# A two-layer graph kernel in fp32 on one core: first slot with zero matmuls ahead of x, second halves of the first rows earlier, and the last statistics in another order

## The chip, the core and the metric

One Trainium2 chip, one of its cores. The time is device microseconds from start to end of one execution; the figure of a kernel is the median of its runs. For the kernel before it is 1274.52 us (three runs, 1274.45 to 1275.23).

## What is computed

The input is `x` (16 x 1024 x 256, fp32) and a symmetric 0/1 matrix `adj` for each of the 16 batches (1024 x 1024). Two layers follow one another, and each ends in a residual sum and a layer norm:

```
e      = leaky(einsum('bid,bjd->bij', x * a0, x))        # slope 0.2
alpha  = where(adj == 1, sigmoid(e), 0)                  # a1..a3 serve adj == 2, 3, 4
x      = layernorm(x + einsum('bij,bjd->bid', alpha, x) + bias)

H      = x @ W
e      = where(adj != 0, exp(-leaky(s[n] + d[m])), 0)    # s = H a_src, d = H a_dst
x      = layernorm(x + elu((e @ H) / rowsum(e)))
```

The kernel has a pass for adjacency of zeros and ones, `one_kind_pass`, which also gathers a flag, and a general pass that only runs if the flag says that another value occurred. With these inputs the general pass does not run.

## The kernel before, in words

**Tiling.** One batch is a slot. A slot's 1024 rows are eight tiles of 128 rows (`NT = 8`), its 256 features two halves of 128 (`ND = 2`), its 1024 columns two halves of 512 (`HALF`). Everything on TensorE is fp32. The order of the instructions on each engine is that of the text: `tc.manual_schedule()` (line 83) leaves no scheduler to move them. Each engine works through its own queue in order, so a waiting instruction holds up what stands behind it.

**Layer 0 of a slot.** `transpose_x` (191) or a blocked load with `turn_x` (184) gives `xT` (features on partitions) and `xa = xT * a0`. For each row tile `jt`, `strip` (205) makes the scores of the tile against the columns from its own on (`pe`, line 219), ScalarE takes tanh twice (227, 228: sigmoid is written as tanh), VectorE takes the larger (229). `finish` (231, the operation is line 235) adds 1, multiplies by the adjacency and writes `al`; POOL puts the diagonal in (245). Since scores and adjacency are symmetric, the part below the diagonal is not computed: in slot 0 `mirror` (268) transposes the blocks on TensorE and VectorE masks them (276). `multiply0` (325, matmul at 332) sums `al` times `x` for one tile of 128 columns of `al`; column tiles 0 to 3 read only the first 512 columns of `al`, tiles 4 to 7 the second 512. `end0` (340) adds the bias and takes the statistics of the layer norm.

**Slot 0's order (504 to 540).** `x` comes in four DMAs, groups of two row tiles: groups 0 and 2 on the SP queue, 1 and 3 on ScalarE's. `a0` comes as a column, 256 elements of 4 bytes, on SP (137), then bias, `a` and `W` (159 to 165), and `x` of slot 1 on SP (513). POOL's queue has four DMAs for the adjacency of slot 0 (quarters: column half by row half) and two for that of slot 1. In `transpose_x` TensorE turns a block into `pxT` (200), VectorE copies it to `xT` (202), ScalarE makes `xa` out of the same PSUM tile (203). Then follow `strip` 0, 1, 2 with `finish` and `mirror` for the first 512 columns, and the loop over eight column tiles `t`: `multiply0(t)`, `strip(t+3)`, `finish(t+2)`, `mirror(t+2)`, then for `t < 4` `finish(0, t, HALF, N)`, the second half of row tile `t`, and `end0(t)`. `make_Wx` (167) in `t = 0, 1` reads `a` and `W`; the blocked load of slot 1's `xT` goes into the same tile as `a` and so waits for it.

**Slots 1 to 15 (542 to 635).** Layer 0 of slot `b` runs beside layer 1 of slot `b-1`: `project` (395), `weights` (439), `sum1` (446), `elu` and `add` (454 to 489).

**The end (638 to 763).** Layer 1 of slot 15. The first three tiles of the result are stored from line 747, tiles 3 and 4 from 753. The last three, 5, 6 and 7 (`N_LAST = 3`), lie in `y_last` and are stored behind the branch on the flag (1108, 1109) in two DMAs on SP: tile 5, then tiles 6 and 7. Tile 7 is made in two half tiles (`end_half`, 705). For tiles 6 and 7 the root is taken on ScalarE (`root`, 641), which loads a table for it, and is inverted with one Newton step on VectorE (646 to 651); two VectorE operations (760) scale the tiles. The statistics of tile 6 are ended by `bn_aggr` in `stats` (288), called from `add` (481) at line 733, ahead of the half tiles of tile 7; those of tile 7 at line 755.

Of the kernel before, what the change touches and what calls it, by code (L numbers as in the profile page):

```python
# [9 lines left out]
F32 = mybir.dt.float32  # L10
# [3 lines left out]
AF = mybir.ActivationFunctionType  # L14
ALU = mybir.AluOpType
# [3 lines left out]
P = 128  # L19
HALF = 512  # L20
# [3 lines left out]
EPS = 1e-5  # L24
LOW = 1.0e-14
CHECKS = 4
N_LAST = 3


@with_exitstack  # L30
def one_kind_pass(
# [33 lines left out]
    nc = tc.nc  # L65
    B, N, D = x.shape
    NT = N // P
    ND = D // P
    HT = HALF // P
    assert ND == 2 and NT == 8 and HT == 4 and N_LAST == 3  # L70

    TINY = 1.0e-36
    const = ctx.enter_context(tc.tile_pool(name="const", bufs=1))
    four = ctx.enter_context(tc.tile_pool(name="four", bufs=4))
    one = ctx.enter_context(tc.tile_pool(name="one", bufs=1))
# [12 lines left out]
    def load_x(b, queues):  # L88
        xs[b] = two.tile([P, NT, D], F32, tag="x", name=f"x_{b}")
        rows = x[b].rearrange("(t p) d -> p t d", p=P)  # L90
        n = NT // len(queues)
        for g, queue in enumerate(queues):
            queue.dma_start(xs[b][:, ts(g, n), :], rows[:, ts(g, n), :])
# [37 lines left out]
        )  # L131


    load_x(0, [nc.sync, nc.scalar, nc.sync, nc.scalar])
    acol = const.tile([P, ND], F32, tag="acol", name="acol")
    with nc.allow_non_contiguous_dma(reason="a column of 256"):
        nc.sync.dma_start(acol, a0.rearrange("(c p) o -> p (c o)", p=P))
    ident = const.tile([P, P], F32, tag="ident", name="ident")
    make_identity(nc, ident)
    ident2 = const.tile([P, P], F32, tag="ident2", name="ident2")  # L140
# [10 lines left out]
    for h in range(2):  # L151
        for g in range(2):
            load_adj(0, g, ts(h, HALF))
    for g in range(2):
        load_adj(1, g)
    power = const.tile([P, NT], F32, tag="power", name="power")
    nc.gpsimd.memset(power, -0.5)
    bias_bc = const.tile([P, D], F32, tag="bias", name="bias_bc")
    nc.sync.dma_start(bias_bc, bias.partition_broadcast(P))

    y_kept = const.tile([P, NT, D], F32, tag="y", name="y_kept")
    a_bc = y_kept[:, 0:2, :].rearrange("p t d -> p (t d)")
    nc.sync.dma_start(a_bc, a[0].partition_broadcast(P))
    Wx = const.tile([P, ND, D + 2], F32, tag="Wx", name="Wx")
    nc.sync.dma_start(Wx[:, :, 2:], W.rearrange("(c p) o -> p c o", p=P))

    def make_Wx(c):

        for s in range(2):
# [21 lines left out]
    def transpose_x(b, g):  # L191

        if g == 0:
            new_xT(b)
            xas[b] = one.tile([P, ND, N], F32, tag="xa", name=f"xa_{b}")
        for c in range(ND):
            pool, tag = ((ps_t, "t"), (ps_acc, "acc"), (ps_acc if c else ps_e, "acc" if c else "e"), (ps_t, "t"))[g]
            pt = pool.tile([P, 2, P], F32, tag=tag, name=f"pxT_{b}_{g}_{c}")
            for t in range(2):
                nc.tensor.transpose(pt[:, t, :], xs[b][:, 2 * g + t, ts(c, P)], ident)  # L200
            flat = pt.rearrange("p t q -> p (t q)")
            nc.vector.tensor_copy(xTs[b][:, c, ts(g, 2 * P)], flat)
            nc.scalar.mul(xas[b][:, c, ts(g, 2 * P)], flat, acol[:, c : c + 1])

    def strip(b, jt):

# [78 lines left out]
    def stats(y, mv, what):  # L285
        st = small.tile([P, nc.vector.BN_STATS_DIM], F32, tag="st", name=f"st_{what}")
        nc.vector.bn_stats(st, y)  # L287
        nc.vector.bn_aggr(mv, st)  # L288

    def rstd(mv, what):  # L290

# [189 lines left out]
    def add(b, t, between=None):  # L481

        y = ys[b][t]
        nc.vector.scalar_tensor_tensor(y, y, 1.0, hs[b, t], ALU.min, ALU.add)
        if (b, t) != (B - 1, NT - 2):
            nc.vector.scalar_tensor_tensor(y, y, -1.0, x1s[b][:, t, :], ALU.add, ALU.add)
        if between:
            between()
        stats(y, mv1s[b][:, t, :], f"1_{b}_{t}")

    def scale1(b, t):
        scale(ys[b][t], *r1s[b][t])

    def store(b, t0, n):
        rows = out[b].rearrange("(t p) d -> p t d", p=P)
        nc.sync.dma_start(rows[:, ds(t0, n), :], y_of[b][:, ds(t0, n), :])

    def acc1(b, t, pool, tag):
        return pool.tile([P, D + 1], F32, tag=tag, name=f"acc1_{b}_{t}")
# [3 lines left out]

    for g in range(NT // 2):
        transpose_x(0, g)
    strip(0, 0)
    strip(0, 1)
    for jt in range(2):
        finish(0, jt, 0, HALF)
        mirror(0, jt)  # L510
        if jt == 0:
            strip(0, 2)
    load_x(1, [nc.sync])
    for t in range(NT):
        multiply0(0, t)
        if t + 3 < NT:
            strip(0, t + 3)
        if t < 2:
            finish(0, t + 2, 0, HALF)
        elif t + 2 < NT:  # L520
            finish(0, t + 2)
        if t + 2 < NT - 1:
            mirror(0, t + 2)
        if t < HT:
            finish(0, t, HALF, N)
        end0(0, t)
        if t < 2:
            make_Wx(t)
        if t == 1:
            new_xT(1)  # L530
            load_blocks(xTs[1], x[1], 0, N)
        if 1 <= t <= CHECKS:
            check_adj(0, t - 1)
        if t in (4, 5):
            scale0(0, 2 * t - 8)
            scale0(0, 2 * t - 7)
            turn_x(1, t - 4)
        if t == 5:
            save_x1(0, 0)
            fetch_x1(0, 0)  # L540
# [97 lines left out]
    last, done = B - 1, B - 2  # L638
    r1s[last] = []

    def root(t):

        v = mv1s[last][:, t : t + 2, 1]
        r = const.tile([P, 2], F32, tag="root", name="root")
        nc.scalar.activation(r, v, AF.Sqrt, bias=eps)  # L645
        nc.vector.reciprocal(r, r)

        n = const.tile([P, 2], F32, tag="newton", name="newton")
        nc.vector.scalar_tensor_tensor(n, v, EPS, r, ALU.add, ALU.mult)
        nc.vector.scalar_tensor_tensor(n, n, -0.5, r, ALU.mult, ALU.mult)  # L650
        nc.vector.scalar_tensor_tensor(r, n, 1.5, r, ALU.add, ALU.mult)
        return r

    n_first = 4
    first = [acc1(last, t, *((ps_e, "e") if t < 3 else (ps_t, "t"))) for t in range(n_first)]
    for m in range(NT):
# [61 lines left out]
    for t in range(end):  # L718
        if n_first - 1 <= t < end - 1:
            multiply1(t + 1)  # L720
        if t == 5:
            multiply_halves()
        if t == 4:
            total = ps_t.tile([P, HT, P], F32, tag="t", name="total")[0:1, 0, 0:1]
            nc.tensor.matmul(total, lhsT=any_bad, rhs=ones, start=True, stop=True)
        elu(last, t, accs[t])
        if 1 <= t < 6:
            add(last, t - 1)
        if t == 5:
            nc.vector.tensor_copy(flag, total)  # L730
            add(last, t)
        if t == 6:
            add(last, t, invert)
        if t in (4, 5):
            r1s[last] += center(mv1s[last][:, ds(3 * t - 12, 3), :], f"1_{last}_{t}")
        if t == 5:
            n_bad = nc.values_load(
                flag, min_val=0, max_val=P, skip_runtime_bounds_check_because="a number of partitions"
            )
        for q in range(2 * t - 4, 2 * t - 2) if 2 <= t < 6 else []:  # L740
            scale1(done, q)
            if q in (3, 7):
                store(done, q - 3, HT)
        if t == 5:
            for q in range(3):
                scale1(last, q)
            store(last, 0, 3)
# [4 lines left out]
    scale1(last, 4)  # L752
    store(last, 3, 2)
    end_half(1)
    nc.vector.bn_aggr(mv1s[last][:, end, :], st_end)
    r = root(6)
    scale1(last, 5)
    for q in (6, 7):
        y = ys[last][q]
        nc.vector.tensor_scalar(  # L760
            y, y, mv1s[last][:, q, 0:1], r[:, q - 6 : q - 5], ALU.subtract, ALU.mult
        )
# [313 lines left out]
def kernel(  # L1076
    tc: tile.TileContext,
    x: bass.AP,
    adjT: bass.AP,
    a0: bass.AP,  # L1080
    a1: bass.AP,
    a2: bass.AP,
    a3: bass.AP,
    bias: bass.AP,
    W: bass.AP,
    a: bass.AP,
    out: bass.AP,
):

    nc = tc.nc
    B, N = x.shape[0], x.shape[1]
    NCHK = B * CHECKS
    with tc.tile_pool(name="flag", bufs=1) as flagp:
        chk = flagp.tile([P, NCHK], F32, tag="chk", name="chk")  # L1100
        fit = flagp.tile([P, B], F32, tag="fit", name="fit")
        y_last = flagp.tile([P, N_LAST, x.shape[2]], F32, tag="y_last", name="y_last")
        n_bad = one_kind_pass(tc, x, adjT, a0, bias, W, a, out, chk, fit, y_last)
        with tc.If(n_bad > 0) as found:
            general_pass(tc, x, adjT, a0, a1, a2, a3, bias, W, a, out)
        with found.Else():
            rows = out[B - 1].rearrange("(t p) d -> p t d", p=P)
            for t, n in ((0, 1), (1, 2)):
                nc.sync.dma_start(rows[:, ds(N // P - N_LAST + t, n), :], y_last[:, ds(t, n), :])


# [35 lines left out]
```

## Time and profile before

| | value |
|---|---|
| median of three runs | 1274.52 us |
| the profiled execution, its own time | 1274.88 us |
| its span, first to last instruction | 1272.9 us |
| TensorE matmuls busy | 1259.1 us (99%) |
| weight loads | 1023.2 us (80%) |
| VectorE | 925.1 us (73%) |
| ScalarE | 651.7 us (51%) |
| POOL | 293.1 us (23%) |
| first matmul starts at | 4.57 us |
| last matmul ends at | 1264.97 us |
| HBM | 151.91 MB read, 60.62 MB written |

The profile comes from one execution. Its own time, 1274.88 us, is 0.36 us above the median of the runs, and 2.0 us of it lie outside the span. In the lines below a matmul in fp32 is two records of the trace, a transpose on TensorE is one. "PEld" is the loading of the stationary operand, which goes on beside a matmul. In a line of the timeline the first number is the start, the second the busy time, in us, `x16` the number of instructions merged into the line; in brackets stands the idle time of the engine ahead of it and what ended it. `SPq`, `ACTq` are a queue issuing DMAs. Matmuls overlap: a record lasts longer than the distance to the next, so the distance is the figure to work with.

### The profile page before, as it was taken

The numbers are of one execution on the slowest core, as the hardware profiler recorded it, in microseconds if no ns is written. First come the engines' busy times: TensorE is split into PE (matmuls) and PEld (weight loads), VectorE is DVE, ScalarE is ACT, GpSimd is POOL, SyncE is SP. The second block draws the span as 40 slices with busy tenths as digits, with TensorE's granted clock in tenths as the row PEclk, the third lists the DMA queues.
The fourth block names the chain that finished last, engine by engine and source line by source line (L and its number), as shares of the span: only waits on it lengthen the run. The fifth ranks groups of instructions, "written<-read, shape, count | busy, mean of one in ns | idle before, by whom it ended". The sixth has DMA issues, their size and how long they took to land.

```text
span 1272.9 us, 17479 instructions
## 1 busy us (share of the span) xinstructions
PE 1259.1 (99%) x5469; PEld 1023.2 (80%) x5469; DVE 925.1 (73%) x2015; ACT 651.7 (51%) x1467; POOL 293.1 (23%) x592
## 2 busy tenths in 40 slices
PE   8999999999999999999999999999999999999997
PEld 6788787887878878788787887878778787887886
DVE  4685877858678686876868868687686867858657
ACT  4544544456454563545645445454455645456434
POOL 2212231212312133121222212223112231212203
PEclk9999999999999999999999999999999999999999
DMA  9379494895948859597694966959579594895312
GB/s 214 72 169 153 87 204 86 179 177 104 192 89 180 170 105 195 92 173 165 131 196 86 179 138 136 194 99 182 119 167 184 99 198 87 176 179 103 100 34 69
DMA packets 604452, 180.24 MB, mean 142 GB/s; under 512 B 481992, under 2 KB 586944, under 8 KB 604352
## 3 DMA queue, kind: packets, MB, share of 16 engines
q1 hardware_dynamic: 583216, 137.03, 54.1%
q0 software_dynamic: 20592, 41.48, 18.3%
q8 instruction: 46, 0.75, 0.2%
q10 hardware_dynamic: 544, 0.52, 0.1%
q14 instruction: 54, 0.44, 0.1%
HBM read 151.91 MB, written 60.62 MB: 167 GB/s over the span
## 4 chain that ended last, share of the span: by engine, by line
PE 98%; DVE 1%; ACT 0%; DMA 0%; issue 0%; ACTq 0%; DVEq 0%
PE acc L332 35%; PE acc L446 34%; PE pe L219 20%; PE pH L395 9%; DMA x<-in_x 0%; PE pxT L200 0%; PE pal L274 0%; PE prow L421 0%; PE pp L414 0%; DVE al L235 0%; ACT y L315 0%; ACT y_kept L315 0%; ACT L645 0%; PE px1T L378 0%; DVE st L287 0%
## 5 line engine op out<-in xcount | busy, mean ns | idle before, releaser
L332 PE MATMUL acc<-x,al 128*128 128x256 f32 x2048 | 445.8, 379 | 1.2 <-DVE al L235 1.2
L446 PE MATMUL acc<-H,e 128*128 128x257 f32 x2032 | 445.3, 380 | 0.0
L446 PEld LDWEIGHTS acc<-H,e 128*128 128x128 f32 x2032 | 384.7, 190 | 57.3 <-DVE e L439 0.6
L332 PEld LDWEIGHTS acc<-x,al 128*128 128x128 f32 x2048 | 387.4, 190 | 53.4 <-DVE al L235 1.6
L219 PE MATMUL pe<-xa,xT 128*128 128x384 f32 (+1 forms) x720 | 251.4, 486 | 0.0
L219 PEld LDWEIGHTS pe<-xa,xT 128*128 128x128 f32 x720 | 133.0, 190 | 81.1 <-issue 42.9
L315 ACT ACTIVATE x<-x,mr,r 128x256 f32<-128x256 f32 x128 | 69.4, 592 | 225.1 <-POOL mr L311 225.1
L439 DVE SCALAR_TENSOR_TENSOR e<-p,pq,adj 128x1024 f32<-128x1024 f32 x128 | 159.7, 1269 | 22.9 <-DMA p<-p_row 19.9
L294 POOL TENSOR_SCALAR ve<-mv 128x4 f32<-128x4 f32 (+2 forms) x49 | 16.8, 344 | 662.9 <-DVE mv L288 658.9
L478 ACT ACTIVATE h<-acc,rinv 128x256 f32<-128x256 f32 x126 | 59.2, 470 | 204.7 <-DVE rinv L470 189.1
L227 ACT ACTIVATE tb<-pe 128x512 f32<-128x512 f32 (+1 forms) x192 | 94.2, 491 | 121.9 <-PE pe L219 93.4
L469 DVE TENSOR_SCALAR rinv<-acc 128x1 f32<-128x1 f32 x127 | 20.0, 157 | 161.9 <-PE acc L446 161.8
L229 DVE TENSOR_TENSOR tb<-tb,low 128x512 f32<-128x512 f32 (+1 forms) x192 | 103.3, 543 | 42.2 <-ACT low L228 42.1
L124 ACT ACTIVATE junk<-adj,minus 128x2048 bf16<-128x2048 bf16 x64 | 127.3, 1989 | 0.0
L395 PE MATMUL pH<-Wx,x1T 128*128 128x258 f32 x512 | 126.3, 381 | 0.0
L395 PEld LDWEIGHTS pH<-Wx,x1T 128*128 128x128 f32 x512 | 97.2, 190 | 35.8 <-issue 14.3
L245 POOL TENSOR_TENSOR al<-ident,al 128x128 f32<-128x128 f32 x128 | 67.8, 530 | 230.4 <-DVE al L235 230.1
L235 DVE SCALAR_TENSOR_TENSOR al<-tb,adj 128x512 f32<-128x512 f32 (+7 forms) x132 | 97.7, 740 | 5.0
L266 DVE SCALAR_TENSOR_TENSOR al<-al,adj 128x512 f32<-128x512 f32 (+3 forms) x150 | 76.9, 537 | 24.2 <-DMA al<-mir 24.2
L228 ACT ACTIVATE low<-pe 128x512 f32<-128x512 f32 (+1 forms) x192 | 93.0, 485 | 0.5 <-DVE tb L229 0.5
L342 DVE SCALAR_TENSOR_TENSOR x<-acc,bias_bc 128x256 f32<-128x256 f32 x128 | 53.8, 420 | 43.7 <-PE acc L332 43.6
L251 DVE STREAM_TRANSPOSE tb<-tb 128x896 f32<-128x896 f32 (+6 forms) x105 | 74.7, 712 | 3.6
(99 smaller groups left out, 942.7 us busy)
## 6 DMA issues: line engine op xcount, KB each, us to landing
adj<-in_adjT POOLq DMA_DIRECT2D x30, 1024.0 KB, 10.1
x_rows<-x SPq DMA_DIRECT2D x31, 512.0 KB, 3.8
x1T<-x_rows SPq DMA_DIRECT2D x248, 64.0 KB, 2.5
x<-in_x SPq DMA_DIRECT2D x15, 1024.0 KB, 6.4
out<-y_kept SPq DMA_DIRECT2D x30, 512.0 KB, 6.6
xT<-in_x SPq DMA_DIRECT2D x112, 128.0 KB, 4.6
p<-p_row POOLq DMA_DIRECT2D x15, 512.0 KB, 4.6
mir<-tb SPq DMA_DIRECT2D x60, 112.0 KB, 3.0
```

Source lines behind the costliest of these rows:

```text
L124: nc.scalar.activation(junk, rows, AF.Square, bias=minus1, scale=2.0, accum_out=chk[:, b * CHECKS + n : b * CHECKS + n + 1],)
L219: nc.tensor.matmul(pe[:, 0:w], lhsT=xTs[b][:, c, ts(jt, P)], rhs=xas[b][:, c, ds(jt * P + o, w)], start=(c == 0), stop=(c == ND - 1),)
L227: nc.scalar.activation(tb[:, ds(o, w)], pe[:, 0:w], AF.Tanh, scale=0.5)
L228: nc.scalar.activation(low[:, 0:w], pe[:, 0:w], AF.Tanh, scale=0.5 * SLOPE)
L229: nc.vector.tensor_tensor(tb[:, ds(o, w)], tb[:, ds(o, w)], low[:, 0:w], ALU.max)
L235: nc.vector.scalar_tensor_tensor(als[b][:, jt, c0:c1], tbs[b, jt][:, c0 - jt * P : c1 - jt * P], 1.0, adjs[b, jt // HT][:, jt % HT, c0:c1] ...
L251: nc.vector.transpose(tb, tb)
L266: nc.vector.scalar_tensor_tensor(v, v, 1.0, rows, ALU.add, ALU.mult)
L332: nc.tensor.matmul(acc, lhsT=als[b][:, jt, ts(t, P)], rhs=xs[b][:, jt, :], start=(jt == 0), stop=(jt == NT - 1),)
L395: nc.tensor.matmul(pt, lhsT=x1Ts[b][:, c, ts(t, P)], rhs=Wx[:, c, :], start=(c == 0), stop=(c == ND - 1),)
L439: nc.vector.scalar_tensor_tensor(es[b][:, m, :], p_bcs[b], pqs[b][:, m, 1:2], adjs[b, m // HT][:, m % HT, :], ALU.mult, ALU.min)
L446: nc.tensor.matmul(acc, lhsT=es[b][:, m, ts(t, P)], rhs=Hs[b][m], start=(m == 0), stop=(m == NT - 1),)
```

## The change

Three places change.

**The front of slot 0.** `a0` is loaded as two rows of 128 on ScalarE's queue, ahead of that queue's two loads of `x`; TensorE turns the rows into two columns and ScalarE copies them to `acol`. VectorE clears a tile of 128 x 128 first of all, and TensorE runs seven fp32 matmuls of it with itself, ahead of the first transpose; their result is not used. In `transpose_x` feature half 0 is now VectorE's alone (copy, then product from the copy) and feature half 1 ScalarE's alone (copy and product, both from PSUM). Slot 1's `x` moves to POOL's queue, between the adjacency of slot 0 and that of slot 1. Bias, `a` and `W` stay on SP, but are issued behind the transposes: a one-column clear of the bias tile by VectorE holds them.

**The loop of slot 0.** The second halves of row tiles 0 to 3 (`finish(0, jt, HALF, N)`) move: those of tiles 0 and 1 stand in `t = 0`, that of tile 2 in `t = 1`, that of 3 in `t = 2`, in each case right behind `multiply0(t)` and ahead of `strip(t+3)`. Before they stood one in each of `t = 0..3`, behind `mirror`.

**The end.** `N_LAST` is 2: tile 5 lies with the tiles before it and is stored on ScalarE's queue right after it is scaled; one DMA on SP is left behind the branch. The `bn_aggr` of tile 6 moves behind that of tile 7, and each of the two has a root of its own on ScalarE (128 x 1 instead of one of 128 x 2). The Newton step stays one for both.

```
-N_LAST = 3
+N_LAST = 2
...
+    arow = two.tile([P, D], F32, tag="h", name="arow")[0:ND, 0:P]
+    nc.scalar.dma_start(arow, a0.rearrange("(c p) o -> c (p o)", p=P))
     load_x(0, [nc.sync, nc.scalar, nc.sync, nc.scalar])
-    acol = const.tile([P, ND], F32, tag="acol", name="acol")
-    with nc.allow_non_contiguous_dma(reason="a column of 256"):
-        nc.sync.dma_start(acol, a0.rearrange("(c p) o -> p (c o)", p=P))
+    zero = two.tile([P, HALF], F32, tag="low", name="zero")[:, 0:P]
+    nc.vector.memset(zero, 0.0)
+    busy = ps_e.tile([P, HALF], F32, tag="e", name="busy")[:, 0:P]
+    for _ in range(N_BUSY):
+        nc.tensor.matmul(busy, lhsT=zero, rhs=zero, start=True, stop=True)
...
+    load_x(1, [nc.gpsimd])
     for g in range(2):
         load_adj(1, g)
+    acol = const.tile([P, ND], F32, tag="acol", name="acol")
+    pcol = ps_e.tile([P, HALF], F32, tag="e", name="pcol")[:, 0:ND]
+    nc.tensor.transpose(pcol, arow, ident[0:ND, 0:ND])
+    nc.scalar.copy(acol, pcol)
...
-            nc.vector.tensor_copy(xTs[b][:, c, ts(g, 2 * P)], flat)
-            nc.scalar.mul(xas[b][:, c, ts(g, 2 * P)], flat, acol[:, c : c + 1])
+            if c == 0:
+                nc.vector.tensor_copy(xT, flat)
+                nc.vector.tensor_scalar(xa, xT, acol[:, 0:1], None, ALU.mult)
+            else:
+                nc.scalar.copy(xT, flat)
+                nc.scalar.mul(xa, flat, acol[:, 1:2])
...
     for g in range(NT // 2):
         transpose_x(0, g)
+    nc.vector.memset(bias_bc[:, 0:1], 0.0)
+    nc.sync.dma_start(bias_bc, bias.partition_broadcast(P))
...
-    load_x(1, [nc.sync])
     for t in range(NT):
         multiply0(0, t)
+        for jt in ([0, 1], [2], [3])[t] if t < 3 else []:
+            finish(0, jt, HALF, N)
         if t + 3 < NT:
             strip(0, t + 3)
...
-        if t < HT:
-            finish(0, t, HALF, N)
         end0(0, t)
...
-    nc.vector.bn_aggr(mv1s[last][:, end, :], st_end)
-    r = root(6)
+    root(end, st_end)
+    root(end - 1, st_full)
+    r = invert_roots()
     scale1(last, 5)
+    store(last, 5, 1, nc.scalar)
...
-            for t, n in ((0, 1), (1, 2)):
-                nc.sync.dma_start(rows[:, ds(N // P - N_LAST + t, n), :], y_last[:, ds(t, n), :])
+            nc.sync.dma_start(rows[:, ds(N // P - N_LAST, N_LAST), :], y_last)
```

`root(t, st)` now ends the statistics and takes one root; `N_BUSY` is 7:

```
    def root(t, st):
        nc.vector.bn_aggr(mv1s[last][:, t, :], st)
        r = roots_sb[:, t - (NT - 2) : t - (NT - 2) + 1]
        nc.scalar.activation(r, mv1s[last][:, t, 1:2], AF.Sqrt, bias=eps)
```

## Prediction, made before the changed kernel was run

> **What bounds the kernel now.** I read the chain that ended last on the page, then who waited on TensorE over the whole span, then the timeline and the chain in pieces at the start, around 40 us and at the end.
>
> ```profile
> PE 98%; DVE 1%; ACT 0%; DMA 0%; issue 0%; ACTq 0%; DVEq 0%
> ```
>
> ```profile
> PE pxT L200 <- DMA x<-in_x: 4.6, 1, 4.6
> PE acc L332 <- DVE al L235: 1.2, 1, 1.2
> ```
>
> TensorE carries the span and waits twice in it: 4.6 us for x, 1.2 us for VectorE. So a change outside TensorE's work can gain only at three places: the front, that wait, and the tail behind the last matmul (1264.97 to 1272.9 us). The change goes to just these.
>
> The front, from the timeline (columns: start, busy us):
>
> ```profile
> 4.57 3.65 PE L200 MATMUL pxT<-ident,x 128*128 128x128 f32 x16 [4.57 <-DMA x<-in_x]
> 6.46 3.03 ACT L203 ACTIVATE xa<-pxT,acol 128x256 f32<-128x256 f32 x8 [3.19 <-DMA acol<-in_a]
> 8.86 0.30 PEld L219 LDWEIGHTS pe<-xa,xT 128*128 128x128 f32 x1 [0.52 <-ACT xa L203]
> 9.40 0.19 PEld L219 LDWEIGHTS pe<-xa,xT 128*128 128x128 f32 x1 [0.24 <-issue]
> 9.83 0.19 PEld L219 LDWEIGHTS pe<-xa,xT 128*128 128x128 f32 x1 [0.24 <-issue]
> 14.98 0.93 PE L274 MATMUL pal<-ident,tb 128*128 128x128 f32 x7
> ```
>
> A weight load starts as the matmul before it starts, so these rows give the pace. The first 128x512 record (8.01 to 8.86) takes 0.85 us, the next 0.54, all later ones 0.43. Sixteen transposes at 4.57 go 0.215 us apart (3.65 less the last one's 0.42, over fifteen), the seven at 14.98 0.11 apart (0.93 less 0.27, over six). TensorE runs at half pace until about 9.1 us. The granted clock, 1.00 in every stretch from 0 to 12 us, does not show this; the pace does. The front is bound by TensorE at half pace: x's four groups land at 4.4, 4.8, 5.9 and 6.2 us (issue plus time to landing, from the view of DMA issues), each ahead of its transposes, and VectorE and ScalarE follow TensorE.
>
> Around 40 us:
>
> ```profile
> 40.36 1.46 PE L332 MATMUL acc<-x,al 128*128 128x256 f32 x6
> 43.06 2.43 PE L332 MATMUL acc<-x,al 128*128 128x256 f32 x10 [1.24 <-DVE al L235]
> ```
>
> Six records at 0.216 would end at 41.66; the next starts at 43.06: 1.40 us lost. VectorE's list has the cause: column tile 4 needs the second half of row tile 3, the last `finish` of its kind (42.18, 0.83 us), behind tanh 6, `finish` 5 and a mirror.
>
> The tail:
>
> ```profile
> 1265.92 1.28 ACT L645 ACT_TABLE_LOAD   x1
> 1267.22 0.29 ACT L645 ACTIVATE root<-mv,eps 128x2 f32<-128x2 f32 x1
> 1267.54 0.17 DVE L646 RECIPROCAL root<-root 128x2 f32<-128x2 f32 x1 [0.75 <-ACT root L645]
> 1268.03 1.96 SPq L1109 DMA_DIRECT2D out<-y_last  x2
> ```
>
> The root waits for the table (to 1267.20), not for the statistics, which end at 1266.80.
>
> **The front, step by step.** The clear on VectorE can start at 0.80, where its first memset stands; 0.15 us (POOL's memset of 128x128: 0.20). Seven fp32 matmuls are 14 records of 128x128; at the half pace of the transposes, 0.215 each, TensorE is busy from 1.05 to 4.05, ahead of x (4.43), so they cost nothing while x lands later than that. Before, the fast pace came 4.5 us after the first work (4.57 to 9.1); the same distance from 1.05 gives 5.6.
>
> Here a rule speaks against the change. The Trainium skill, "TensorE: Matmul & The Clock Gate", Part 1 (The HAM clock gate), wants some 3.4 us of sustained work, watched in a free-running window; Part 4 (PE-mode transpose) adds that transposes do not count as busy in the same way. The filler is 3.0 us, and what follows it is transposes: by the rule the clock rises 3.4 us after the first real matmul, no gain. The trace disagrees on the second half: the pace rose 1.1 us after the first matmul (8.01) and 4.5 after the first transpose, so transposes count here. By the rule the front gains 0, by the row what follows. I take the row, with the window's free phase as uncertainty: the rise lies between 4.5 and 7.9 (1.05 plus one to two windows). Whether matmuls of zeros count no row shows.
>
> With the rise at 5.6: four or five transposes at 0.215 to 5.6, the rest at 0.11, but now x holds them. ScalarE issues groups 1 and 3 0.49 us later, behind the rows of a0 (a 1 KB load, which I expect at 3 to 4, and it hides unless it is later than x). I put group 1 at 4.8 to 5.2, group 3 at 6.2 to 6.6. The last transpose is through at about 7.05. Evacuation per group: VectorE copy 0.43 and product 0.41 less some overlap (the row of line 760, 0.41, two at 0.33), from 5.25: the first two groups by 6.9, four by 8.5. ScalarE two operations at 0.36, from 5.7: 7.2 and 8.7; the acol wait is gone. So the first score matmul starts at 7.05; its second pass needs ScalarE's product at 7.9, the second chunk (8.8) needs 8.7. Eight records at 0.43 end at 10.5. Before they ended at 8.01 + 0.85 + 0.54 + 6 x 0.43 = 11.98. Gain **1.45** us; with the rise at 7.9 it is 0.55, with the rise ahead of x about 1.75.
>
> **What that moves up.** From there to 40 us TensorE has no wait, and its suppliers move with it, save the DMAs. First row half of the adjacency, first column half: landed 13.2, its second quarter 17.5, used at 17.63. That would stop VectorE if `mirror` came 1.45 earlier. But in 8 to 21 us the DMA engines were full (share 1.17), shared with bias, a, W and slot 1's x; these go behind (x behind four quarters on POOL's queue, the others past 8.5). I estimate quarters at 9.5, 14, 16.5, 19, from 512 KB in about 2.6 us alone (24.1 less 21.4, the last quarter). Moved loads: slot 1's adjacency landed at 29 and 34 and may come at 27 to 33, first used at 61.8; bias, a, W at 13 to 14, used from 27.6; POOL's memset, one issue (0.8 us) later, used at 44.4. All covered.
>
> **The loop.** The halves of tiles 0 and 1 now stand where VectorE was idle 3.38 us ahead of 24.83: 2 x 0.61. Tile 2's stands in the 1.35 ahead of 31.63, tile 3's in the 0.31 ahead of 36.60 plus the 0.6 freed earlier. Each fits; without cover, tanh 3 to 5 would wait 0.6 to 1.2, and TensorE has some 4 us of slack to their mirrors. Behind `multiply0(4)` nothing late remains: its rows 4 and 5 are done at 38.3. The stall's 1.40 goes, and 0.11 of slow restart with it (10 records, 43.06 to 45.33 against 2.16). Gain **1.5**. Next late would be slot 1's scores at 56.2 - 2.95 = 53.2; their `xa` (53.15) follows the same VectorE chain, about 3 earlier, 50.1.
>
> **The tail.** Tile 6's `bn_aggr` (0.18) leaves a place where VectorE waited for ScalarE anyway (`h_end`, 1264.2): 0 gain. Behind tile 7's it lies under the table load: 0 cost. Two roots instead of one: a 128x1 step follows another on ScalarE by 0.06 (lines 403, 404), a 128x2 by 0.2: cost 0.06 to 0.2, on the path. Tile 5's store leaves SP, which was free from 1268.4 to 1269.10, so its issue did not delay the last one. But the last store took 0.89 to issue and 2.7 to land, one of equal size at 1265.46 0.37 and 2.4: from 0 to -0.3. On ScalarE's queue nothing waits behind tile 5's store; issue to landing 4.0 to 4.9 there (x at the start) would end at 1272.2 to 1273.1 against 1271.8, its SP row of 2.8 at 1271.0. I take SP's row, since nothing else moves then. Sum **0** (-0.3 to +0.4; +1.3 with the slow end).
>
> **Sum.** On the profiled execution: 1274.88 - 1.45 - 1.5 + 0 = 1271.9. The median is 0.36 lower, which I carry: **1271.6**.
>
> **Rivals.**
> A. As summed: 1271.6, within 1270.9 to 1272.3.
> B. The filler does not lift the clock (zeros, or too short). The front stays bound by half pace; only the loop gains: 1274.5 - 1.5 = 1273.0. For it: the rule. Against: transposes counted. A hidden VectorE wait that eats the loop's gain would give the same time.
> C. Better phase and the quicker last store: 1.75 + 1.5 + 0.3: 1271.0. For it: 4.5 us is longer than one window.
> D. Slower: the rows of a0 land late, and all transposes stand behind the transpose of these rows on TensorE. Small loads have a near row: the old column took 4.6 us and landed at 6.37, behind x on its queue. The new one is first on its queue, against this. Every us past 4.43 shifts the front by one, at half pace; from 1.5 later, 5.9, the loop's gain is gone and it turns slower. At 6.37: 1274.5 + 1.95 - 1.5 = 1275.0; at 8, 1276.6.
> That the change does nothing to the stall is ruled out by the order on VectorE: the awaited `finish` stands ahead of tanh 5, one pass of the loop before the place where it was late.
>
> **Chances.** A 0.61, C 0.14, B 0.20, D 0.05. A measurement can tell about 0.2%, 2.5 us: below 1272.0 is faster. Of A 0.48 lies below it, with C 0.62 faster; 0.13 of A and B 0.33 same; slower, D, 0.05. Range 1270.6 to 1273.3: A, C and B with its 0.3 of tail.
>
> **What would show it.** Records of `busy` from about 1.05 to 4.05; `pxT` distance 0.11 for groups 2 and 3; the first `pe` near 7.05 and 0.43 from its first record; `acol` ready ahead of 4.6. No wait of `acc` on `al` in TensorE's list; `multiply0(4)` in one piece. First adjacency quarter at about 9.5. From the last matmul to the end still 7.9. Wrong would be: `pe` at 0.85 again (B), `pxT` waiting for `arow` (D), a new wait in slot 1.

## The result and the profile after

The changed kernel takes 1273.18 us (median of 16 runs, 1272.12 to 1274.70) against 1275.06 for the kernel before (16 runs, 1274.11 to 1275.99) in the same session. The ratio of the runs is 0.9983, with a 95% interval of 0.9977 to 0.9989. By the two medians it is 1.88 us less where 2.9 were forecast (1274.52 less 1271.6). The prediction took 0.2%, 2.5 us, as the least that can be told: by that bound the result is "same", to which it gave 0.33, and not "faster", to which it gave 0.62. The profiled execution took 1273.82 (span 1271.7, before 1272.9) and lies above its median; this matters below.

The waits of TensorE, and the chain by engine:

```profile
PE pxT L203 <- DMA x<-in_x: 1.6, 1, 1.6
PE busy L143 <- DVE ones L153: 1.0, 1, 1.0
```

```profile
PE 98%; DMA 1%; DVE 0%; ACT 0%; issue 0%; ACTq 0%; DVEq 0%
```

The wait of `acc` for `al` is gone. The 1.0 of `busy` is the start of the kernel, up to the first matmul of zeros. The wait for x went from 4.6 to 1.6, but this 1.6 is new: it stands in the middle of the transposes, and it puts a DMA into the chain. The front in the timeline:

```profile
1.04 3.36 PE L143 MATMUL busy<-zero 128*128 128x128 f32 x14 [1.04 <-DVE ones L153]
4.33 0.26 PE L166 MATMUL pcol<-ident,arow 2*128 2x2 f32 x1
4.52 2.31 PE L203 MATMUL pxT<-ident,x 128*128 128x128 f32 x12
8.44 0.63 PE L203 MATMUL pxT<-ident,x 128*128 128x128 f32 x4 [1.61 <-DMA x<-in_x]
8.91 4.46 PE L227 MATMUL pe<-xa,xT 128*128 128x512 f32 x10
12.35 0.19 PEld L227 LDWEIGHTS pe<-xa,xT 128*128 128x128 f32 x1 [0.24 <-issue]
```

The fourteen records of zeros run as forecast, a0's rows are there in time, and twelve transposes follow. Then TensorE stands for 1.61 us: the fourth group of x, issued at 1.78, lands at 8.31. Its line in the view of DMA issues (KB, us from issue to landing; before it was 4.95 us, from 1.25 to 6.20):

```profile
x<-in_x ACTq DMA_DIRECT2D x1, 256.0 KB, 6.5
```

The first score matmul starts at 8.91 (before 8.01), at full pace from its first record. The row at 12.35 is the weight load that starts as the eighth score record ends; before it was 11.98. So in this execution the front lost 0.37 us. Around 40 us:

```profile
40.73 3.62 PE L342 MATMUL acc<-x,al 128*128 128x256 f32 x16
```

Column tile 4, its sixteen records in one piece, without the stall. The tail:

```profile
1264.81 1.28 ACT L666 ACT_TABLE_LOAD   x1
1266.10 0.48 ACT L666 ACTIVATE root<-mv,eps 128x1 f32<-128x1 f32 x2
1266.62 0.17 DVE L671 RECIPROCAL root<-root 128x2 f32<-128x2 f32 x1 [0.88 <-ACT root L666]
1268.17 0.37 SPq L1136 DMA_DIRECT2D out<-y_last  x1
```

The two roots take 0.48 where one of two columns took 0.29, still behind the table; the last store's issue takes 0.37 where it took 0.89. From the last matmul (1263.84) to the end of the span are 7.86 us, before 7.93.

### The profile page after: what moved, and what is told of

Its sections match the earlier page's. It is cut to its first block, busy times and chain, and to the rows that moved or that the text cites. A ratio compares the mean times of both kernels' runs of the same rounds, so it can differ in the third digit from the quotient of the medians.

```text
span 1271.7 us, 17514 instructions
## 1 busy us (share of the span) xinstructions
PE 1261.2 (99%) x5484; PEld 1025.7 (81%) x5484; DVE 924.9 (73%) x2017; ACT 651.4 (51%) x1469; POOL 293.5 (23%) x593
## 4 chain that ended last, share of the span: by engine, by line
PE 98%; DMA 1%; DVE 0%; ACT 0%; issue 0%; ACTq 0%; DVEq 0%
PE acc L342 35%; PE acc L456 35%; PE pe L227 19%; PE pH L405 9%; DMA x<-in_x 1%; PE pal L282 0%; PE prow L431 0%; PE pp L424 0%; ACT y L325 0%; ACT y_kept L325 0%; ACT L666 0%; PE px1T L388 0%; DVE y L494 0%; PE pxT L203 0%; ACTq L136 0%
```

## The experiments

Theory 1: the front's gain was eaten because the fourth group of x, issued half a microsecond later on ScalarE's queue behind a0's rows (1.78 against 1.25), is still out when the adjacency's packets begin. Rivals: the adjacency alone, the queue alone, the small load alone, or a clock that does not rise. All ratios are to the kernel before, run beside each on the same chip, with the 95% interval; the medians of the kernel before in the three sessions are 1275.30, 1275.26 and 1275.18. The intervals are about 0.2% wide and overlap, so differences of half a microsecond between medians are not clear of the noise. What is said below of causes rests on one trace of each kernel and on the spread of its runs; the medians only agree.

The table gives, for each profiled execution, the landing of the last group of x, the end of the eighth score record, the end of the last matmul, the distance between these two, and the time from the last matmul to the span's end (us).

| kernel | x in | eighth ends | last matmul | between | tail | own time |
|---|---|---|---|---|---|---|
| before | 6.20 | 11.98 | 1264.97 | 1253.00 | 7.9 | 1274.88 |
| change | 8.31 | 12.35 | 1263.84 | 1251.49 | 7.9 | 1273.82 |
| third group on SyncE | 6.03 | 10.51 | 1262.00 | 1251.49 | 8.1 | 1272.18 |
| adjacency later | 6.03 | 10.64 | 1262.14 | 1251.50 | 8.0 | 1272.37 |
| no zeros | 6.34 | 13.03 | 1264.53 | 1251.49 | 8.0 | 1274.57 |
| old front | 6.36 | 12.49 | 1263.98 | 1251.49 | 7.7 | 1273.80 |
| change again | 7.00 | 11.04 | 1262.53 | 1251.49 | 8.2 | 1272.78 |
| a0's rows on SyncE | 6.16 | 10.69 | 1262.19 | 1251.50 | 8.0 | 1272.32 |
| SyncE and one root | 6.01 | 10.53 | 1262.02 | 1251.49 | 7.9 | 1272.00 |
| loop only | 6.41 | 12.74 | 1264.23 | 1251.50 | 8.4 | 1274.71 |
| no load of a0 | 6.45 | 10.52 | 1262.01 | 1251.49 | 7.9 | 1272.03 |
| the same, issued late | 8.28 | 12.31 | 1263.80 | 1251.49 | 8.2 | 1274.14 |
| SyncE, root, adjacency | 6.00 | 10.65 | 1262.15 | 1251.50 | 8.2 | 1272.47 |

Behind the eighth record every execution with the moved `finish` takes 1251.49 or 1251.50, and the one without it 1253.00. All that differs besides is the front and the tail, which takes 7.7 to 8.4 us.

**The fourth group of x issued as SyncE's third** (in the table "third group on SyncE").

```
-    load_x(0, [nc.sync, nc.scalar, nc.sync, nc.scalar])
+    load_x(0, [nc.sync, nc.scalar, nc.sync, nc.sync])
```

> The last group of x is issued as third on SyncE's queue instead of second behind the rows of a0 on ScalarE's. Theory 1 (its place behind the rows of a0 on ScalarE's queue made it late): it lands at 6.0 to 6.6 us instead of 8.31, TensorE's 1.6 us wait for x goes, the first score matmul starts at 7.1 to 7.4 instead of 8.91, and the time is 1.5 us below the change's, about 2.9 to 3.4 below the kernel before. Theory 2 (the adjacency's packets, which now start at 5.2 us, hold up whatever part of x is still out): it still lands at 7.5 to 8.3, and the time stays within 0.5 us of the change's.

1272.18 us (1272.06 to 1272.81, 10 runs), 0.9978 (0.9968 to 0.9987), 3.1 below the kernel before. TensorE's rows:

```profile
4.52 0.67 PE L203 MATMUL pxT<-ident,x 128*128 128x128 f32 x4
5.43 1.53 PE L203 MATMUL pxT<-ident,x 128*128 128x128 f32 x12 [0.24 <-DMA x<-in_x]
6.97 6.38 PE L227 MATMUL pe<-xa,xT 128*128 128x512 f32 x15
```

The fourth group is in at 6.03:

```profile
x<-in_x SPq DMA_DIRECT2D x1, 256.0 KB, 4.3
```

The 1.6 us wait for it is gone; the 0.24 left is for ScalarE's one group (in at 5.39). Scores start at 6.97, and the eighth record ends at 10.51, 1.46 ahead of before. The group was issued hardly earlier (1.73 against 1.78). So a late issue alone is not the cause: it needs ScalarE's queue.

**The adjacency later.**

```
+    for i in range(2):
+        nc.gpsimd.memset(pause[:, i, :], 0.0)
     for h in range(2):
         for g in range(2):
             load_adj(0, g, ts(h, HALF))
```

> Two clears of 128x1024 on GpSimd ahead of the first adjacency load delay all loads of that queue by some 1.5 to 2.5 us; the adjacency's packets then start at about 7, behind x, as in the kernel before (6.6). Theory 1 (place behind the rows of a0): the last group of x still lands at about 8, no gain over the change. Theory 2 (adjacency meets x): it lands at 6.2 to 6.6, the wait of 1.6 us goes, the score matmuls start at 7.1 to 7.4, and the time is 1.5 us below the change's unless the later adjacency (first quarter then at 12 to 13 us) makes VectorE's first finish wait at about 13.

1272.42 us (1271.96 to 1272.93, 11 runs), 0.9978 (0.9969 to 0.9987). With ScalarE's queue and a0's rows as in the change, x is in at 6.03, and one of the eleven runs lies over 1272.9 (of the change's, 15 of 27, below). So the adjacency is a needed part too. But the expectation had its first packets at about 7 us, and they came at 5.38 (change 5.21), though issued 1.8 us later (3.67 against 1.88). What changed is how many there are while x ends: from 5 to 6 us (packets, MB, share of 16 engines; q0 is POOL's queue, with the adjacency), here and then in the change:

```profile
q0 software_dynamic: 21, 0.02, 80.0%
```

```profile
q0 software_dynamic: 94, 0.10, 57.7%
```

The first quarter landed at 9.45 (change 10.81); nothing waited for it.

**The change without the zeros.**

```
-    for _ in range(N_BUSY):
-        nc.tensor.matmul(busy, lhsT=zero, rhs=zero, start=True, stop=True)
```

> The change without the fourteen records of zeros (nothing of the result depends on them). If the zeros lifted the clock: transposes of x again 0.215 us apart, score matmuls at 0.85 at first, half pace until about 9, and since the last group of x still lands at about 8.3, the eight first score records end 0.4 to 0.8 us later than in the change, which is what the time shows. If the transposes did it, or the clock's window, and not the zeros: fast pace at 6.2 again and the change's time.

1274.28 us (1272.81 to 1276.38, 11 runs), 0.9991 (0.9982 to 1.0).

```profile
3.53 1.11 PE L198 MATMUL pxT<-ident,x 128*128 128x128 f32 x4 [1.11 <-DMA x<-in_x]
5.84 2.82 PE L198 MATMUL pxT<-ident,x 128*128 128x128 f32 x12 [1.20 <-DMA x<-in_x]
```

Twelve transposes in 2.82 us are half pace, all of them; the first score records are 0.85 apart and the pace rises near 10.8. The zeros do lift the clock. The last group of x landed at 6.34 here, though its queue and the adjacency's were as in the change: its lateness changes from execution to execution, and the 8.3 expected for this run was wrong.

**The old front with the new loop and end.** The kernel before with the moved `finish`, the two roots and the stores.

> The kernel before with the moved halves of finish and the new end, but the old front (column of a0 on SyncE's queue, no zeros, bias, a and W early, VectorE and ScalarE sharing as before). Theory (the loop carries the whole gain, the front none while its last group of x is late): 1.5 to 1.6 us below the kernel before, within 0.5 us of the change. Rival (the front gains 1.45 on most executions, and only the profiled one had the late x; then loop or end give less): only 0.4 to 0.8 us below the kernel before.

1273.77 us (1273.15 to 1274.13, 11 runs), 0.9988 (0.9979 to 0.9997): 1.53 below the kernel before. The change gained 1.88, so by the medians its front is worth some 0.35 as it stands (0.8 by its second set of runs, below), less than these runs can tell; the kernel with SyncE's third group gained 3.12, so the front is worth 1.6 when x is in time.

**The change once more.**

> The changed kernel itself once more, for its spread and a second trace of its front. Theory (the last group of x is late in some executions and on time in others, because on ScalarE's queue behind the rows of a0 it is still out when the adjacency starts): times spread over 2 us or more, from 1272.1 to about 1274.5, median 1.0 us above that of the kernel with the third group on SyncE; the trace shows either about 8 us and a wait of some 1.5 us on TensorE, or about 6.2 and none, with the run's time to match. Rival (the first trace was typical and fixed): 8.3 again and a narrow spread round 1273.5.

1272.91 us (1272.07 to 1273.97, 11 runs), 0.9982 (0.9973 to 0.9991), 2.35 below the kernel before. The trace shows a third landing, 7.00, with waits of 0.45 (for ScalarE's first group, in at 5.57) and 0.43 and scores from 7.60. Of the change's 27 runs here and above 15 lie over 1272.9; of the ten with the third group on SyncE none.

**a0's rows on SyncE's queue, behind its first group of x.** ScalarE then issues its groups of x at 0.73 and 1.26, as in the kernel before.

```
-    nc.scalar.dma_start(arow, ...)
             queue.dma_start(xs[b][:, ts(g, n), :], rows[:, ts(g, n), :])
+            if (b, g) == (0, 0):
+                nc.sync.dma_start(arow, ...)
```

> The rows of a0 are loaded between the two groups of x on SyncE's queue, so that ScalarE's queue issues its two groups of x at 0.73 and 1.25 us as in the kernel before; SyncE's second group is issued 0.5 us later. Theory 1 (the half microsecond behind the rows of a0 made ScalarE's last group late): both last groups are in by 6.4 us, time within 0.5 us of 1272.2, narrow, if the rows of a0 are in by about 4.5; each us later costs one. Theory 2 (ScalarE's queue as such loses against the adjacency): the fourth group still lands at 7 to 8.3 in some executions, spread over 2 us, about 1273.2. Third case: the rows of a0 land at 5 or later behind x, every transpose waits, and it is slower by that.

1272.79 us (1272.25 to 1274.79, 11 runs), 0.9985 (0.9976 to 0.9994). Inconclusive: the profiled execution has x at 6.16 and a wait of 0.55 for a0's rows, but four runs lie over 1274 and no trace shows why. Late rows of a0 or a late second group on SyncE's queue (issued at 1.63 instead of 1.22) are both open.

**The load of a0 taken out, early and late issue.** Rows of a0 set to 0.05, so the kernel leaves out a0's values; then the same with ScalarE's first group held until 1.43 by a clear of part of its tile (SyncE's two groups go at 0.73 and 1.22 as before).

```
-    nc.scalar.dma_start(arow, ...)
+    nc.vector.memset(arow, 0.05)
```

```
+        if b == 0:
+            nc.vector.memset(xs[b][:, ts(1, n), 0:192], 0.0)
```

> The change without the load of a0's rows: they are set to 0.05 on VectorE, so the scores differ from the reference. ScalarE's queue then issues its two groups of x at 0.73 and 1.25 us, and the adjacency starts at about 5.1 us as in the change. Theory 3 (the small load ahead of x in the same queue makes the tail of that queue lag by some half a microsecond, and the lagging packets then meet the adjacency): all of x in by 6.1, no wait on TensorE, times narrow round 1272.1. Theory 1 (only the later issue counts): the same here. Theory 2 (ScalarE's queue as such loses against the adjacency): the last group at 7 to 8.3 in many executions, spread of 2 us, about 1273.

> As the kernel without the load of a0's rows, but ScalarE's first group of x waits for a clear of a part of its tile on VectorE, so that its issue begins at about 1.3 to 1.4 us as in the change, with no small load ahead of it. Theory 1 (the late issue): the last group of x is late again, spread of 2 us, about 1273. Theory 3 (the small load itself): in by 6.3, narrow, within 0.3 us of the kernel with early issue.

Early: 1272.34 us (1272.03 to 1272.50, 11 runs), 0.9979 (0.9970 to 0.9988), x in at 6.45. Late: 1273.01 us (1272.51 to 1275.50, 11 runs), 0.9986 (0.9977 to 0.9995), x in at 8.28. Over 1272.9 lie none of the early kernel's eleven runs and nine of the late one's. DMA queues from 6 to 8.5 us (q10 is ScalarE's, q0 POOL's; packets, MB, share of 16 engines), the late kernel first:

```profile
q0 software_dynamic: 356, 0.36, 103.4%
q10 hardware_dynamic: 27, 0.02, 3.7%
```

In the early one:

```profile
q0 software_dynamic: 478, 0.48, 119.2%
q10 hardware_dynamic: 1, 0.00, 0.0%
```

In the change:

```profile
q0 software_dynamic: 386, 0.39, 104.8%
q10 hardware_dynamic: 17, 0.02, 2.2%
```

With the third group on SyncE's queue only the adjacency is left:

```profile
q0 software_dynamic: 400, 0.40, 110.1%
```

ScalarE's queue carries 544 packets for x, 512 of 1 KB and the rest of 4 bytes. The last 17 of them in the change, 27 in the late kernel and 6 in the change's second trace (x in at 7.00) start behind 6 us, among the adjacency's. Where x was in time, its last packets start 0.04 us apart, one after another, as in the kernel without zeros (5.59 to 5.97); in the change there is a gap from 5.93 to 6.52, and then many are 0.13 apart, as all are in the second trace (5.76 to 6.55).

Theory 3 (the small load itself) falls: the tail is there without any load of a0. Theory 2 (ScalarE's queue as such) falls too, since with early issue it is narrow. What stays is theory 1 (the late issue) in a narrower form: ScalarE's queue, with two groups issued half a microsecond late, and the adjacency beside them. Where one of the three is taken away, x was in by 6.0 to 6.5 in the trace; that is not proof by itself, since the kernel without zeros had 6.34 with all three, so the spreads (none of ten, one of eleven and none of eleven over 1272.9) carry it. Two things stay open. Why is it just this queue, when SyncE's third group, issued as late, was in time? And why did the kernel with a0's rows on SyncE's queue, where ScalarE issues early, still have five runs of eleven over 1272.9, four of them over 1274?

**Loop only; one root; all together.** The kernel before with the moved `finish` alone; the SyncE kernel with one 128x2 root behind both statistics; the same with one clear on GpSimd ahead of the adjacency.

```
-        nc.scalar.activation(r, mv1s[last][:, t, 1:2], AF.Sqrt, bias=eps)
+        if t == NT - 2:
+            nc.scalar.activation(roots_sb, mv1s[last][:, t:, 1], AF.Sqrt, bias=eps)
```

> The kernel before with nothing changed but the place of the second halves of finish. Theory: TensorE's wait of 1.2 us for al goes and with it 1.5 us, the whole of what the kernel with the old front gained (1.53), so the new end is worth nothing within 0.3 us. Rival: the loop gives only 1.2 or less and the end the rest.

> The third group on SyncE's queue, and one root of 128x2 behind both statistics, as in the kernel before; tile 5's store stays on ScalarE's queue. Theory: the same front as with the third group alone (1272.2), and from the last matmul to VectorE's last scaling 0.2 us less (4.10 instead of 4.30), 1272.0. Rival: the root waits for the second statistic longer than a 128x1 root for the first, and nothing is gained.

> The third group of x on SyncE's queue, one root, and one clear of 128x1024 on GpSimd ahead of the adjacency, which then starts about 0.9 us later. Theory: x is safe by two means, so the time is that of the kernel with the first two, 1272.1, or up to 0.2 below it with a narrower spread. Rival: the later adjacency makes VectorE wait for its first quarter, and it is slower by up to 0.5 us.

Loop only: 1273.81 us (1273.16 to 1274.71, 11 runs), 0.9988 (0.9979 to 0.9997), 1.45 below the kernel before; with the new end it was 1.53, so the end is worth nothing that these runs can tell. One root: 1272.09 us (1271.88 to 1272.97, 11 runs), 0.9976 (0.9967 to 0.9985); from the last matmul to VectorE's last scaling 4.13 us against 4.31 with two roots. All together: 1272.26 us (1271.93 to 1272.83, 11 runs), 0.9977 (0.9968 to 0.9986): the later adjacency adds nothing to the group on SyncE. The kernel with SyncE's third group and one root has the lowest median: 0.8 us under the change in the same session, 3.2 under the kernel before (1275.26).

## Why the prediction was right or wrong

- **The loop, 1.5: right.** 1253.00 less 1251.49 is 1.51, and by time alone 1.45. The four halves found room where they were put, and the next suspect (slot 1's scores) did not become late: no such wait stands in TensorE's list.
- **The tail, 0: right as a sum.** Two roots cost 0.18, the upper end of the 0.06 to 0.2; the last store, issued in 0.37 instead of 0.89, landed in 2.4 instead of 2.7. Tile 5's store cost nothing that shows.
- **The clock: right in kind.** The zeros lift it, and transposes keep it busy: in the loop-only kernel the pace rose 2.2 us after the first score matmul and 5.65 after the first transpose. The rule of the Trainium skill that the prediction set against the row ("TensorE: Matmul & The Clock Gate", Part 4, PE-mode transpose) would have meant no gain; the measurement decides for the row. The rise came 3.1 to 5.1 us after the first record of zeros, at 4.15 to 6.16, against 5.6 taken and 4.5 to 7.9 allowed; even at 6.13 (the one-root kernel) it cost 0.1 at most, since x paces the transposes by then.
- **The front, 1.45: wrong in this kernel, and here is the failed step.** The prediction put "group 3 at 6.2 to 6.6" (the fourth group, counted from 0), from the old landing, 6.20, and the 0.49 us of later issue. In the changed kernel it measured 8.31 and 7.00 and, without the zeros, 6.34. It had also written that the adjacency would land earlier (9.5 for the first quarter; 10.81 measured), and costed only what that would displace behind it, not what was still ahead of it. The adjacency's first packets came at 6.6 to 7.1 us with the old front and at 4.8 to 5.3 with the new one, at the same issue time, 1.88; perhaps because the column of a0, bias, a and W no longer stood in SyncE's queue, which was not tried. So it started sooner, on top of an x whose last group was issued later. Where x was in time behind the zeros, the sum holds: the eighth score record was forecast to end at 10.5 and ended at 10.51 to 10.69.
- **The front's mean worth** was 0.35 instead of 1.45 by the medians of the runs that give the result, which is the missing 1 us (0.8 in the second set). The predicted median was off by 1.6; the other half microsecond is the base, 1275.06 in the runs beside the change against 1274.52 in the three that were shown.
- **The rivals, and luck.** B named the measured time (1273.0) for a reason that did not occur. The sum itself (A, up to 1272.3) missed it; the stated range, up to 1273.3, takes it in only because B was counted in, so that is luck. D, a0's rows landing late, did not occur in the change; its cousin, x landing late because it is issued behind a0's rows, did, and no rival named it.

## What to carry to other kernels

A load put ahead of others in one queue can cost more than its issue time: here half a microsecond of later issue became some 2 us of later landing in one trace and 0.8 in another, on ScalarE's queue, when the end of these loads met the first packets of the adjacency from POOL's queue; on SyncE's queue it did not. So ask for each load what is still out when the next stream starts, and when early loads are taken out of the way, look at what moves up into their place. A spread that grows with a change (2.6 us here, against 1.9 before and 0.8 with the third group on SyncE) is a hint at such a race, and a second trace is worth more than a finer reading of the first.

## What the runs showed that was not expected

- Behind the front TensorE's work took 1251.49 to 1251.50 us in twelve executions with different loads and ends, so what differs between these executions lies in the first 13 us and the last 8.
- The last 6 to 27 packets of x held up TensorE by 0.4 to 1.7 us, at a time when the DMA engines carried the adjacency, whose first quarter TensorE did not wait for in any of these traces.
- The adjacency's first packets hardly followed its issue. With the third group on SyncE's queue they came at 5.01; with the adjacency issued 0.89 us later as well, at 5.12; and issued 1.8 us later than in the change (5.21), at 5.38.
- The granted clock in the profile's rows showed 1.00 throughout the front, because these rows count the time ahead of the first clock record as full speed. The record itself, in each packed trace, has the step: it starts at 9.07 us in the kernel before and at 6.16 in the change, where the pace doubles. With the old front it came 4.5, 5.0 and 5.65 us after the first transpose; without zeros, where TensorE stood for 1.2 us in between, 7.2 after the first transpose and 4.9 after work went on at 5.84.
- In all thirteen traces the stretch at full clock lasts 1256.11, 1259.52 or 1262.93 us, which are 3.41 apart: the clock changed in steps of such a grid, not at once with the work. This fits the rise coming anywhere between 4.15 and 6.16 us although the zeros always start at 1.04.
- A clear of 128x1024 on GpSimd delayed the issue on its queue by 0.89 us; a clear of 128x384 on VectorE took 0.38.
